# Two graph-attention layers on one core: rank products, list counting, row scatters and the last block's small tile moved

## The chip, the cores and the metric

The kernel runs on one core of one Trainium2 chip. The metric is the device time of one execution in microseconds (us). Before the change the median of three runs is 1944.09 us (1942.63 to 1948.15). The profile is of one further execution of 1946.15 us, whose recorded span, from the first to the last instruction, is 1944.3 us.

## The reference

Two layers of the same form are applied to 2708 tokens of width 512, in float32, with an adjacency matrix of 0 and 1 that has some eight neighbours in a row:

```
mask   = adj + eye(n)
q,k,v  = h @ Wq.T + bq, h @ Wk.T + bk, h @ Wv.T + bv      # 8 heads of 64
scores = q . k / sqrt(64), -1e9 where mask == 0
ctx    = softmax(scores) @ v
h1     = layer_norm(h + ctx @ Wo.T + bo)
h2     = layer_norm(h1 + relu(h1 @ W1.T + b1) @ W2.T + b2)  # hidden width 2048
```

All tokens pass through every product; attention needs only the few neighbours of a token.

## The kernel before

**Tiles.** Tokens are handled in 22 tiles of 128; the last (number 21) has 20 tokens. Products of such a small tile are made as "quarters": four products share the array, each in 32 of the output's 128 partitions, and the vector engine adds the four parts (`plus_rest`, L583).

**Keys, values and lists.** `first` (L832) makes keys and values of layer 0, tile by tile, adds the key bias on the vector engine (L879) and writes the rows to a table in memory (L885). Beside this, `lists` (L670) finds for each token the places of its neighbours in the adjacency matrix. `counted` (L699) counts every token's list and sums the counts over the tiles, some 30 vector-engine instructions ending with L746; before, it is called as soon as the last tile's lists are made, in the loop over the tiles.

**Ranks.** Tokens are then regrouped by length of list, so that a tile needs as many steps as its longest list. `ranked` (L756) turns the counts into places: four products (L763, L770) over a triangular matrix and a matrix of ones, a multiply and a sum on the vector engine (L777, L783), and a conversion (L785). With the places, GpSimd scatters the lists tile by tile to memory (L789, 22 indirect transfers), reads them back in the new order (L808, L801), and takes from them the old number of each new token (`ident_i`, L819). `own_rows` (L961) then gathers rows of the input for the first tiles of attention; TensorE transposes them and makes their queries (`own_query`, L972). Gathers of keys and values (L1004) follow.

**Queries.** `first_queries` (L903) makes the queries of layer 0 for all tiles (L922), which the vector engine scales and adds the bias to (L929), and which are written to memory. In it `ranked` is called after the first tile's product. After tile 12, `listed(True)` (L834) makes the first lists of places usable (L827), and at tile 13 the own queries are made.

**Attention and feed-forward.** Tiles are worked in 11 pairs (`blocks`, L1432), the last being the small tile 21 with tile 8. `attend` (L1437) multiplies gathered keys by the query on the vector engine, takes the exponential on the scalar engine and adds up weighted values; it is advanced step by step inside the loops of feed-forward. `feed_forward` (L1311) makes 16 chunks of the hidden layer (L1351), applies ReLU on the scalar engine (L1359), and adds each chunk into one accumulator per tile (`second`, L1324), three chunks late (`LAG`); for a small tile `quarters` (L1339) does this once per four chunks. Then come the sum with the residual (L1375), the norm (`norm`, L1147, with one power on GpSimd), and in the last layer a scatter of the rows to the output (L1379). In layer 0, `keys_values` (L1390) makes the next layer's keys and values and scatters them to the next table (L1417).

**Order.** The orders of TensorE, of the scalar engine and of SP's transfer queue are as written. GpSimd's is as written up to the last block of layer 0; the vector engine's only in `first_queries` and at the start of layer 1. Elsewhere a planner orders these two when the kernel is built. Two writes to one table are put in order by default: the later one waits on GpSimd until the earlier has landed. For the rank scatters this is declared needless already:

```
tc.declare_no_dep(move.ins, group="moved", reason="no two tokens have one rank")
```

Of the kernel before, what the change touches and what calls it, by code (L numbers as in the profile page):

```python
# [18 lines left out]
P = 128  # L19
# [453 lines left out]
def by_edges(ctx: ExitStack, tc: tile.TileContext, x, xT, adj, layers, out, good):  # L473
# [130 lines left out]
    def lists_of(pa):  # L604
# [151 lines left out]
        def ranked(hot, before, half):  # L756

            at = pa.tile([P, NT], F32, tag="at", name="at", bufs=1)
            for h in range(2):
                ts = slice(h * half, (h + 1) * half)  # L760
                pr = ps.tile([P, DM], F32, tag="g", name="pr")
                w = half * LIST
                nc.tensor.matmul(  # L763
                    pr[:, :w],
                    tri,
                    hot[:, ts, :].rearrange("p t e -> p (t e)"),
                    start=True,
                    stop=False,
                )
                nc.tensor.matmul(  # L770
                    pr[:, :w],
                    ones,
                    before[:, ts, :].rearrange("p t e -> p (t e)"),
                    start=False,
                    stop=True,
                )
                nc.vector.tensor_tensor(  # L777
                    hot[:, ts, :].rearrange("p t e -> p (t e)"),
                    hot[:, ts, :].rearrange("p t e -> p (t e)"),
                    pr[:, :w],  # L780
                    ALU.mult,
                )
                nc.vector.tensor_reduce(at[:, ts], hot[:, ts, :], AX.X, ALU.add)  # L783
            ranks = pa.tile([P, NT], I32, tag="ranks", name="ranks", bufs=1)
            nc.vector.tensor_copy(ranks, at)  # L785
            moved = []
            for t in range(NT):
                r = size(t)
                move = nc.gpsimd.indirect_dma_start(  # L789
                    out=rec_d[:, :],  # L790
                    out_offset=bass.IndirectOffsetOnAxis(ap=ranks[:r, t : t + 1], axis=0),
                    in_=rec[:r, t, :],
                    in_offset=None,
                    bounds_check=N - 1,
                    oob_is_err=False,
                )
# [11 lines left out]
            rest = nc.gpsimd.dma_start(out=new[:LW, last, :], in_=rec_d[last * P :, :])  # L808
# [10 lines left out]
            nc.gpsimd.tensor_copy(ident_i[:, first:], new[:, first:, LIST])  # L819
# [12 lines left out]
    def first(w, meanwhile):  # L832
# [39 lines left out]
        for t in range(NT):  # L872
# [4 lines left out]
            if t == 0:  # L877
                finish(turning)
            nc.vector.tensor_tensor(kv[:r, :DM], k[:r], bk[:r], ALU.add)  # L879
            plus_rest(kv[:r, :DM], k, r)  # L880
            v = project(xs, r, wv, "v", other=True)
            nc.scalar.copy(kv[:r, DM:], v[:r])
            plus_rest(kv[:r, DM:], v, r)
            if before:
                nc.scalar.dma_start(**before)  # L885
            before = dict(out=kv_d[0][t * P : t * P + r, :], in_=kv[:r])
            if t == 0:
                finish(load())
            while done < min(NT, 1 + LEAD * t):
                lists(done)  # L890
                done += 1
                if done == NT:
                    counts = counted()
            meanwhile(t)
            if t == QT:
                wq = matrix(w, "Wq", "wq")
# [6 lines left out]
    def first_queries(bq, wq, counts, ranked, listed, pa, tokens, meanwhile):  # L903
# [14 lines left out]
        for t in range(NT):  # L918
# [1 line left out]
            if t % 2 == 0 and made:  # L920
                written()
            q = project(tokens(t, 1), r, wq, "q", other=t % 2 > 0)  # L922
            if t == 0:
                ranked(*counts)
                xrs = [own_rows(g) for g in order[:3]]
            if t % 2 == 0:
# [45 lines left out]
    def own_query(g, zT, to, bq, wq):  # L972
# [3 lines left out]
        nc.vector.scalar_tensor_tensor(to[:r], q[:r], DK**-0.5, bq[:r], ALU.mult, ALU.add)  # L976
        plus_rest(to[:r], q, r, DK**-0.5)

    def checked():

        sc = at.tile([P, LIST, NH], F32, tag="sc", name="checks", bufs=2)
# [19 lines left out]
            nc.sync.dma_start(out=to[:r], in_=table[g * P : g * P + r, :])  # L1001

    def gather(to, table, s):
        nc.gpsimd.indirect_dma_start(  # L1004
            out=to,
            out_offset=None,
            in_=table[:, :],
# [106 lines left out]
            return cx  # L1114

    places = []

    def rows_of_keys(n):

# [12 lines left out]
    def loads(n):  # L1132

        ready = []
        for g, s0, c in (chunk for g in order for chunk in chunks_of(g)):
            r = size(g)
            kv = rows_of_keys(n)
            for s in range(s0, s0 + c):
                gather(kv[:r, s - s0, :], kv_d[n], idx[:r, g, s : s + 1])
            ready.append(kv)  # L1140
            if len(ready) > EARLY:
                yield ready.pop(0)
# [32 lines left out]
    class Layer:  # L1175
# [135 lines left out]
        def feed_forward(self, block, hs, hT):  # L1311

            w = sum(size(g) for g in block)
            accs = [ps_a.tile([P, DM], F32, tag=f"a{i}", name=f"a{i}") for i in range(len(block))]
            fts = []

            def second(f, only=None):
                c0 = 0
# [29 lines left out]
            for f in range(NFC):  # L1348
                pf = ps_f.tile([P, DM], F32, tag="f", name="pf")
                for c in range(NC):  # L1350
# [20 lines left out]
            zs = []  # L1371
            for g, a, h in zip(block, accs, hs):
                r = size(g)
                z = h
                nc.vector.tensor_tensor(z[:r], a[:r], h[:r], ALU.add)  # L1375
                plus_rest(z[:r], a, r)
                norm(z, r, self.g2, self.e2)
                if self.n == NL - 1:
                    nc.gpsimd.indirect_dma_start(  # L1379
                        out=out,  # L1380
                        out_offset=bass.IndirectOffsetOnAxis(ap=ident_i[:r, g : g + 1], axis=0),
                        in_=z[:r],
                        in_offset=None,
                        bounds_check=N - 1,
                        oob_is_err=False,
                    )
                zs.append(z)
            yield zs

        def keys_values(self, block, zs):  # L1390
# [23 lines left out]
                yield  # L1414
            for i, g in enumerate(block):
                r = size(g)
                nc.gpsimd.indirect_dma_start(  # L1417
                    out=kv_d[n][:, :],
                    out_offset=bass.IndirectOffsetOnAxis(ap=ident_i[:r, g : g + 1], axis=0),
                    in_=kvs[:r, i, :],  # L1420
                    in_offset=None,
                    bounds_check=N - 1,
                    oob_is_err=False,
                )
            yield

# [280 lines left out]
```

## Time and profile before

| what | value |
|---|---|
| median of three runs | 1944.09 us |
| profiled execution, its span | 1946.15 us, 1944.3 us |
| TensorE busy | 1858.4 us, 96% of the span |
| vector engine busy | 1321.0 us, 68% |
| scalar engine busy | 934.7 us, 48% |
| GpSimd busy | 809.3 us, 42% |
| mean granted TensorE clock | 0.981 |
| transfers | 366.92 MB, mean 189 GB/s |

PE is TensorE, PEld its weight load, DVE the vector engine, ACT the scalar engine, POOL GpSimd, SP the engine that only issues transfers. A line of the time line gives the start, the length, the engine, the line in the kernel, the operation, what it writes and reads, and how many instructions in a row are merged; in brackets stands the idle time of the engine before it and what ended it. Lengths of neighbouring lines can overlap, as instructions are pipelined. A float32 product shows as two instructions (passes). The granted clock is 1 at full speed.

### The profile page before, as it was taken

How to read it: one execution, taken by the hardware profiler on the slowest of the kernel's cores; microseconds unless marked ns; L12 is line 12 of the kernel's file. 1: busy time of each engine (PE TensorE's matmuls, PEld its weight loads, DVE VectorE, ACT ScalarE, POOL GpSimd, SP SyncE). 2: the span in 40 equal slices, each digit the busy share in tenths (PEclk: the TensorE clock that was granted, in tenths of full speed). 3: DMA queues.
4: the chain of work that ended last, by engine and by line, in shares of the span. 5: the costliest groups of instructions: out<-in, count | busy, mean ns of one | idle time of the engine just before them, and what ended most of it. 6: DMA issues, size and time to landing. Idle time of an engine off the chain costs nothing. (4 is left out here: it accounts for less than half of the span.)

```text
span 1944.3 us, 20898 instructions
## 1 busy us (share of the span) xinstructions
PE 1858.4 (96%) x6162; PEld 1096.7 (56%) x6162; DVE 1321.0 (68%) x2172; ACT 934.7 (48%) x3219; POOL 809.3 (42%) x710
## 2 busy tenths in 40 slices
PE   9998968999999999999999997999999999999996
PEld 4443435556656556665665553566666666666663
DVE  5885467768759687695841237696987998877421
ACT  4660236445546655574451113555475767654510
POOL 3113526535536555364410124344555775546101
PEclk9999979999999999999999998999999999999998
DMA  9998848555646656554401478656665766643000
GB/s 322 355 314 299 275 136 302 172 179 184 205 138 201 217 188 197 177 183 154 146 17 65 136 246 325 202 197 204 203 222 168 251 222 220 209 155 125 17 6 14
DMA packets 131486, 366.92 MB, mean 189 GB/s; under 512 B 16668, under 2 KB 37004, under 8 KB 128654
## 3 DMA queue, kind: packets, MB, share of 16 engines
q0 software_dynamic: 69120, 246.35, 38.0%
q1 hardware_dynamic: 53332, 99.66, 14.8%
q10 hardware_dynamic: 8910, 19.48, 2.6%
q8 instruction: 50, 0.82, 0.2%
q14 instruction: 74, 0.61, 0.1%
HBM read 314.62 MB, written 50.83 MB: 188 GB/s over the span
## 5 line engine op out<-in xcount | busy, mean ns | idle before, releaser
L1004 POOL DMA_INDIRECT kv<-kv_d,idx x420 | 547.0, 1302 | 452.2 <-DVE acc L1080 273.5
L1351 PE MATMUL pf<-hT,w 128*128 128x256 f32 (+1 forms) x2816 | 637.2, 373 | 7.2 <-ACT ft L1359 5.2
L1324 PE MATMUL a<-w,ft 128*128 128x512 f32 x1344 | 632.2, 596 | 5.3 <-ACT ft L1359 4.4
L1351 PEld LDWEIGHTS pf<-hT,w 128*128 128x128 f32 x2816 | 521.2, 191 | 186.6 <-issue 106.5
L1359 ACT ACTIVATE ft<-pf,b 128x256 f32<-128x256 f32 (+1 forms) x352 | 160.3, 460 | 458.5 <-PE pf L1351 458.3
L1041 DVE TENSOR_TENSOR kv<-kv,q 128x1024 f32<-128x1024 f32 (+3 forms) x222 | 254.2, 1157 | 169.2 <-DMA kv<-kv_d,idx 131.1
L1324 PEld LDWEIGHTS a<-w,ft 128*128 128x128 f32 x1344 | 253.2, 191 | 198.6 <-issue 171.6
L1067 ACT ACTIVATE kv<-kv,p 128x64 f32<-128x64 f32 x1232 | 311.0, 335 | 5.0
L1047 DVE TENSOR_REDUCE sc<-kv 128x16 f32<-128x1024 f32 (+3 forms) x222 | 253.8, 1153 | 1.5
L1080 DVE TENSOR_TENSOR acc<-acc,kv 128x1024 f32<-128x1024 f32 (+2 forms) x178 | 204.0, 1146 | 18.9 <-ACT kv L1067 17.0
L1156 POOL TENSOR_TENSOR rd<-va,mhalf 128x1 f32<-128x1 f32 (+1 forms) x88 | 90.4, 1028 | 274.6 <-DVE va L1154 273.7
L576 PE MATMUL o<-wo,cT 128*128 128x512 f32 x336 | 151.1, 602 | 0.5 <-ACT cT L1171 0.5
L1073 DVE TENSOR_TENSOR kv<-kv,p 128x512 f32<-128x512 f32 (+1 forms) x178 | 121.4, 682 | 34.6 <-ACT p L1060 34.6
L1060 ACT ACTIVATE p<-sc,minus 128x8 f32<-128x8 f32 x420 | 102.8, 294 | 69.2 <-DVE sc L1047 62.1
L1111 ACT ACTIVATE cx<-acc,su 128x64 f32<-128x64 f32 (+1 forms) x352 | 88.5, 334 | 74.7 <-DVE su L1103 57.6
L576 PEld LDWEIGHTS o<-wo,cT 128*128 128x128 f32 x336 | 64.5, 193 | 83.2 <-issue 72.9
L681 ACT ACTIVATE code<-aj 128x2708 bf16<-128x2708 int32 (+1 forms) x22 | 73.3, 3332 | 49.2 <-POOL aj L677 49.0
L684 DVE MAX8 tops<-code 128x8 f32<-128x247 f32 (+2 forms) x242 | 83.1, 401 | 19.3 <-ACT code L681 19.3
L1160 DVE SCALAR_TENSOR_TENSOR h<-h,rd,ln_b 128x512 f32<-128x512 f32 (+1 forms) x88 | 65.6, 747 | 40.6 <-POOL rd L1156 40.6
L1067 ACT ACTIVATE acc<-kv,p 128x64 f32<-128x64 f32 (+1 forms) x352 | 88.8, 334 | 1.4
L1410 ACT COPY kvs<-v 128x512 f32<-128x512 f32 (+1 forms) x22 | 12.9, 586 | 158.9 <-PE v L576 138.5
L1375 DVE TENSOR_TENSOR h<-a,h 128x512 f32<-128x512 f32 (+1 forms) x44 | 29.9, 679 | 85.2 <-PE a L1339 48.8
(154 smaller groups left out, 1560.2 us busy)
## 6 DMA issues: line engine op xcount, KB each, us to landing
aj<-in_adj SPq DMA_DIRECT2D x21, 1354.0 KB, 8.4
kv_d<-kvs ACTq DMA_DIRECT2D x21, 512.0 KB, 7.4
w<-in_W SPq DMA_DIRECT2D x20, 512.0 KB, 6.5
xg<-in_xT SPq DMA_DIRECT2D x19, 512.0 KB, 8.6
kv<-kv_d,idx POOLq DMA_INDIRECT x420, 5.8
w<-in_W ACTq DMA_DIRECT2D x12, 512.0 KB, 7.2
q_d<-qs SPq DMA_DIRECT2D x22, 256.0 KB, 3.4
zT_d<-zT SPq DMA_DIRECT2D x22, 256.0 KB, 4.3
```

The lines of the kernel that those rows point to most:

```text
L576: nc.tensor.matmul(o[:r], xs(c), wm[:, c, :], start=(c == 0), stop=(c == NC - 1))
L1004: nc.gpsimd.indirect_dma_start(out=to, out_offset=None, in_=table[:, :], in_offset=bass.IndirectOffsetOnAxis(ap=s, axis=0), bounds_check=N ...
L1041: nc.vector.tensor_tensor(kv[:r, :c, :DM], kv[:r, :c, :DM], self.q[:r].unsqueeze(1).to_broadcast([r, c, DM]), ALU.mult,)
L1047: nc.vector.tensor_reduce(self.sc[:r, s0 : s0 + c, :], kv[:r, :c, :DM].rearrange("p s (h d) -> p s h d", d=DK), AX.X, ALU.add,)
L1060: nc.scalar.activation(p[:r, s, :], self.sc[:r, s, :], AF.Exp, bias=minus[:r, g, s : s + 1])
L1067: nc.scalar.activation(to[:, i, hd], kv[:r, i, DM + h * DK : DM + (h + 1) * DK], AF.Copy, scale=p[:r, s0 + i, h : h + 1],)
L1073: nc.vector.tensor_tensor(to[:, 0, :].rearrange("p (h d) -> p h d", d=DK), kv[:r, 0, DM:].rearrange("p (h d) -> p h d", d=DK), p[:r, s0, : ...
L1080: nc.vector.tensor_tensor(self.acc[:r, :c, :], self.acc[:r, :c, :], kv[:r, :c, DM:], ALU.add)
L1156: nc.gpsimd.tensor_tensor(rd[:r], va[:r], mhalf[:r], ALU.pow)
L1324: nc.tensor.matmul(a[:r], fts[f][:, c0 : c0 + r], self.w2[f // 2][:, f % 2, :], start=(f == 0), stop=(f == NFC - 1),)
L1351: nc.tensor.matmul(pf[:, :w], self.w1[f // 2][:, c, f % 2 * P : f % 2 * P + P], hT[:, c, :w], start=(c == 0), stop=(c == NC - 1),)
L1359: nc.scalar.activation(ft[:, :w], pf[:, :w], AF.Relu, bias=self.b1[:, f : f + 1])
```

## The change

Four things are changed.

1. `counted` is called in the last turn of the loop over key tiles, behind that tile's key bias and value copy and ahead of the additions of its quarters. Before, it was called when the last lists had been made, some turns earlier.
2. `ranked` is called after the second tile's query product, not the first's. Its two output banks are those of the feed-forward accumulators (`ps_a`, tags a0 and a1) and no longer taken in turn with the queries' (`ps`, tag g).
3. The scatters of key and value rows, and of output rows, go through a new function `put`, which declares that they need no order among themselves. The first gather from a table is made to wait for all its scatters by hand.
4. In the last block of the last layer (`apart`) all 16 hidden chunks are made first and kept, in two tiles of the pool of gathered keys; the quarters of the small tile run after every fourth chunk. The small tile's sum, norm and scatter are written first, and the 16 products of the full tile after them.

```
-                pr = ps.tile([P, DM], F32, tag="g", name="pr")
+                pr = ps_a.tile([P, DM], F32, tag=f"a{h}", name="pr")
...
             nc.vector.tensor_tensor(kv[:r, :DM], k[:r], bk[:r], ALU.add)
-            plus_rest(kv[:r, :DM], k, r)
             v = project(xs, r, wv, "v", other=True)
             nc.scalar.copy(kv[:r, DM:], v[:r])
-            plus_rest(kv[:r, DM:], v, r)
             if before:
                 nc.scalar.dma_start(**before)
+            if t == NT - 1:
+                counts = counted()
+            plus_rest(kv[:r, :DM], k, r)
+            plus_rest(kv[:r, DM:], v, r)
...
                 lists(done)
                 done += 1
-                if done == NT:
-                    counts = counted()
...
             q = project(tokens(t, 1), r, wq, "q", other=t % 2 > 0)
-            if t == 0:
+            if t == 1:
                 ranked(*counts)
                 xrs = [own_rows(g) for g in order[:3]]
...
+    def put(table, s, rows, group):
+
+        move = nc.gpsimd.indirect_dma_start(
+            out=table[:, :],
+            out_offset=bass.IndirectOffsetOnAxis(ap=s, axis=0),
+            in_=rows,
+            in_offset=None,
+            bounds_check=N - 1,
+            oob_is_err=False,
+        )
+        tc.declare_no_dep(move.ins, group=group, reason="no two tokens have one place")
+        tc.add_to_no_dep_group(group, move.ins)
+        return move
...
+                load = gather(kv[:r, s - s0, :], kv_d[n], idx[:r, g, s : s + 1])
+                for move in written[n]:
+                    tc.add_manual_dep(
...
+                written[n].clear()
...
+            apart = self.n == NL - 1 and block == blocks[-1]
...
-                ft = dn.tile([P, 2 * P], F32, tag="ft", name="ft", bufs=4)
+                if apart:
+                    ft = wide[f // 8][:, f % 8, :]
+                else:
+                    ft = dn.tile([P, 2 * P], F32, tag="ft", name="ft", bufs=4)
...
-                if f >= LAG:
+                if f >= LAG and not apart:
                     second(f - LAG)
...
-            for g in block:
+            if apart:
+                quarters(NFC - 1)
+            for g in () if apart else block:
...
                 r = size(g)
+                if apart:
+                    for f in range(NFC):
+                        second(f, g)
                 z = h
                 nc.vector.tensor_tensor(z[:r], a[:r], h[:r], ALU.add)
...
-                    nc.gpsimd.indirect_dma_start(
...
+                    put(out, ident_i[:r, g : g + 1], z[:r], "out")
...
-                nc.gpsimd.indirect_dma_start(
...
+                written[n].append(
+                    put(kv_d[n], ident_i[:r, g : g + 1], kvs[:r, i, :], f"kv{n}")
                 )
```

More of the change, by code (lines that the diff above doesn't have):

```diff
@@ L1003, in gather @@
     def gather(to, table, s):
-        nc.gpsimd.indirect_dma_start(
+        return nc.gpsimd.indirect_dma_start(
             out=to,
@@ L1116, in by_edges @@
     places = []
+    written = [[] for _ in range(NL)]
     def rows_of_keys(n):
@@ L1138, in loads @@
             for s in range(s0, s0 + c):
-                gather(kv[:r, s - s0, :], kv_d[n], idx[:r, g, s : s + 1])
+                load = gather(kv[:r, s - s0, :], kv_d[n], idx[:r, g, s : s + 1])
+                for move in written[n]:
+                    tc.add_manual_dep(
+                        load.ins,
+                        move.ins.name,
+                        mybir.DependencyInfo(
+                            mybir.DependencyClass.Sync, mybir.DependencyReason.DATA
+                        ),
+                        reason="every row of keys is in its place",
+                    )
+                written[n].clear()
             ready.append(kv)
@@ L1315, in feed_forward @@
             fts = []
+            apart = self.n == NL - 1 and block == blocks[-1]
+            if apart:
+                wide = [
+                    at.tile([P, SLOTS, 2 * DM], F32, tag="kv", name="fts", bufs=KVB)
+                    for _ in range(2)
+                ]
+                wide = [t.rearrange("p s (i w) -> p (s i) w", w=2 * P) for t in wide]
             def second(f, only=None):
@@ L1373, in feed_forward @@
                 r = size(g)
+                if apart:
+                    for f in range(NFC):
+                        second(f, g)
                 z = h
@@ L1378, in feed_forward @@
                 if self.n == NL - 1:
[L1379 to L1386, printed above, removed]
+                    put(out, ident_i[:r, g : g + 1], z[:r], "out")
                 zs.append(z)
@@ L1416, in keys_values @@
                 r = size(g)
[L1417 to L1423, printed above, removed]
+                written[n].append(
+                    put(kv_d[n], ident_i[:r, g : g + 1], kvs[:r, i, :], f"kv{n}")
                 )
```

## The prediction

> **What bounds the kernel now.** I read the page's head, then who TensorE waited for, then the order of events at the three places that the change touches. From the page, and from TensorE's list of waits (total, times, longest, in us):
>
> ```profile
> PE 1858.4 (96%) x6162; PEld 1096.7 (56%) x6162; DVE 1321.0 (68%) x2172; ACT 934.7 (48%) x3219; POOL 809.3 (42%) x710
> PE tp L1166 <- ACT cx L1111: 25.5, 4, 14.2
> ...
> PE q L576 <- DVE kvs L879: 6.1, 1, 6.1
> ...
> PE tp L1166 <- DMA xr<-in_x,ident_i: 0.3, 1, 0.3
> ```
>
> TensorE sets the time nearly everywhere. Its idle time is 86 us, and from 1230 us to 1925 us it waits only 4.5 us in all. So a faster GpSimd or vector engine in the middle buys nothing; only the start (lists, ranks, first attention), the boundary of the layers and the tail can move the end. The start, in order of time (start, length, engine and line, in brackets the idle time before and what ended it):
>
> ```profile
> 160.83 0.71 DVE L746 TENSOR_TENSOR before<-before,run 128x528 f32<-128x528 f32 x1
> 161.46 1.87 DVE L879 TENSOR_TENSOR kvs<-k,bk 128x512 f32<-128x512 f32 x3
> 162.20 6.43 PE L576 MATMUL q<-wq,xg 128*128 128x512 f32 x8 [6.07 <-DVE kvs L879]
> 168.47 0.61 PE L763 MATMUL pr<-hot,tri 128*128 128x264 f32 x2
> 169.56 0.43 DVE L777 TENSOR_TENSOR hot<-hot,pr 128x264 f32<-128x264 f32 x1 [1.92 <-PE pr L770]
> 171.85 1.10 POOL L789 DMA_INDIRECT rec_d<-rec,ranks  x1 [20.29 <-DVE ranks L785]
> 172.70 0.69 DVE L929 SCALAR_TENSOR_TENSOR qs<-q,bq 128x512 f32<-128x512 f32 x1 [1.14 <-DMA kv_d<-kvs]
> 203.05 0.59 POOL L808 DMA_DIRECT2D new<-rec_d  x1 [3.05 <-DMA rec_d<-rec,ranks]
> 209.00 1.10 POOL L1004 DMA_INDIRECT xr<-in_x,ident_i  x1 [0.65 <-POOL ident_i L819]
> 215.32 1.85 PE L1166 MATMUL tp<-ident,xr 128*128 128x128 f32 x12 [0.28 <-DMA xr<-in_x,ident_i]
> 227.51 0.69 DVE L929 SCALAR_TENSOR_TENSOR qs<-q,bq 128x512 f32<-128x512 f32 x1 [2.13 <-PE q L576]
> 263.15 1.91 PE L1166 MATMUL tp<-ident,cx 128*128 128x128 f32 x4 [14.21 <-ACT cx L1111]
> ```
>
> Three things to see. The key biases (L879) run behind the counting (L746), and TensorE loses 6.07 us to that. From the rank products at 168.47 a chain without play leads on: ranks, 22 scatters on GpSimd at 1.28 us each, the lists back, the rows of the first own queries, and their transposes at 215.32, which already wait 0.28 us. And the next big pause, 14.21 us, is for attention that starts from the same lists. The tail:
>
> ```profile
> 1923.86 0.68 DVE L1375 TENSOR_TENSOR h<-a,h 20x512 f32<-20x512 f32 x1 [28.02 <-PE a L1339]
> 1926.01 0.69 DVE L1375 TENSOR_TENSOR h<-a,h 128x512 f32<-128x512 f32 x1
> 1931.96 1.16 POOL L1379 DMA_INDIRECT out<-h,ident_i  x1 [0.57 <-DVE h L1160]
> 1936.58 1.01 POOL L1379 DMA_INDIRECT out<-h,ident_i  x1 [3.47 <-issue]
> ```
>
> Both norms of the last block share the vector engine, and the second scatter stands 3.47 us with nothing to do but see the first land.
>
> **What the Trainium skill says.** "TensorE: Matmul & The Clock Gate", What's actually happening: after about one idle window of 3.4 us the array falls to half rate until it has been busy for a window. The trace agrees: after the pause of 6.07 us eight passes took 6.43 us, where tiles of eight passes are 3.43 us apart later. "DMA: Bandwidth & Descriptors", Anatomy of one DMA: a transfer has about 2 us of fixed cost, mostly the receipt of the write; here a row scatter of the output lands 2.7 to 3.8 us after issue, so that is what a wait between two scatters costs. "TensorEngine Tiling (Array Packing)", Key Properties: changing the tiling mode drains the array; here the quarter products (20-row tile) begin 0.09 us after the last product's modelled end, 0.5 us later than the next load would have.
>
> **The change part by part.** The changed kernel can be built, so the order of its instructions on each engine is known.
>
> Counting behind the key biases: on the vector engine nothing moves. Its order there is the planner's; in the changed build the two full biases and the small one still follow the last add of the counting. The 6.07 us pause and the half-rate query behind it stay: 0. (If it had moved, up to 6 us plus some 3 us of half clock were to be had.)
>
> Rank products behind the second query: they stay ready before 168.47, so nothing is gained by waiting; they move back by one query, 3.43 us, and the multiply (169.56) could start at 172.99. But the vector engine has a fixed order here, and the scaling of query 0 now stands ahead of it. That waits for the write of the last keys to leave its buffer, which held until 172.70, and takes 0.69 us: the multiply starts at 173.4, 3.85 us later. Ranks, 22 scatters, lists back, own rows and key gathers (213.36) all follow on GpSimd in order: +3.85 each. TensorE's pause of 0.28 us becomes about 4.1. Own rows may land faster than then: before, they shared the queues with a query write and a load issued at 208.93 and 209.39, now these have a head start. Taken: -0.7 (0 to -1.9). A pause near 4 us costs clock: after 3.66 us at 285 the clock stood at 0.5 until about 290.6, after 3.75 us at 658.8 for about 3.5 us; half of 3.5 to 5.4 us is 1.7 to 2.7. The query multiplies behind it are on the path, since the vector engine waits for them (2.13 us at 227.51) before attention's second step. Taken +1.7 (0 to 3.3). Sum +4.8, ends +2 and +7.2. Could the 14.21 us pause absorb this? No: what it waits for is late by the same amount. The two other accumulator banks for the products cost nothing: no query behind the products waited for a bank.
>
> Row scatters independent: in layer 0 the second scatter of a pair mostly waits for the scalar engine's copy of the values, not for the first (403.73 and 409.30; 558.22 and 566.83). At the boundary the last one goes at 1156.05, released by the copy that ends at 1155.77, and the first gather waits 2.59 us for its landing as before. The added waits of that gather on all lanes are semaphore reads of about 0.04 us. In layer 1 GpSimd is freed a little while TensorE has no wait. Taken 0; -1 to +0.5. Were TensorE not full there, a pair could be worth up to 3 us.
>
> Last block: TensorE now does all 16 hidden chunks, each fourth followed at once by quarter products, and then 16 products of the full tile. Before, a full-tile product lay between a hidden chunk and the quarters and covered the ReLU. Chunk 7 of before: products start 1902.59, ReLU 1903.85 to 1904.23. With 0.2 us to wake TensorE the quarters start 1.84 us after the chunk's start and take 0.99: 2.83 us, against 1.007 for a plain chunk. 12 x 1.007 + 4 x 2.83 + 16 x 0.857 + 0.27 (drain) = 37.4 us from 1890.92: TensorE ends at 1928.3, not 1925.65, +2.65. But the small tile's add, norm and scatter now lie under the last 13.7 us of products. For the full tile alone, the block before shows 3.97 us from add (1888.55) to scatter (1892.52); plus 0.2 for two small copies between: add at 1928.45, scatter at 1932.65, instead of 1936.58: -3.9. The 7.7 us from there to the end of the span stay. Ends: -6.6 if the ReLU wait is nothing, -2 if it is nearly twice as long. The hidden tiles lie in key buffers last filled at 1780 us: no wait.
>
> Sum: +4.8 + 0 + 0 - 3.9 = +0.9. The profiled execution took 1946.15 (span 1944.3 and 1.85 around it), so 1947.05; it was 2.06 above the median of the three runs, so against that 1945.0. About 0.3%, 5.8 us, is what can be told from no change.
>
> **Rivals.** (1) Slower, about 1951. The write of the last keys, now ahead of the rank multiply, lands late. It took some 4.5 us from issue (167.67, 0.53 us) to 172.70, where such writes have a median of 7.4; every us later is one more on the chain. At 7.4 it is +2.9, and with the clock at its upper end the start costs 9.3. It decides once the start costs over 9.7. For: the queues are full from 166 to 186 us. Against: what is in flight then is unchanged. (2) Faster, about 1937.5: the rank chain hides its delay, as rows and lists land quickly on queues that then have less to carry, and the ReLU is covered after all: 0 - 6.6. For: the DMA share at 208 to 210 us is only 0.10. Against: transposes wait already. (3) The tail gives nothing, as the ReLU waits eat it: +4.8, 1949; still no difference by the measure.
>
> **How the numbers follow.** The sum above 0.58, rival 1 0.20, rival 2 0.12, rival 3 0.10. Rival 3 and the sum lie inside 0.3% but for a few in a hundred at the slow side; so faster 0.12, same 0.66, slower 0.22. The range for 8 in 10 runs from 1938 (just short of rival 2) to 1951.5 (the ends +7.2 and -2 give +5.2, 1949.3; rival 1 reaches past it).
>
> **What would show it.** Pause before the first query multiply again near 6 us; first rank scatter near 175.7; transposes of own rows waiting near 3 to 4 us with clock 0.5 behind it; first context transposes of the second tile near 268; tail with the last scatter some 7.7 us before the end, no wait before it, and pauses of about 0.5 us ahead of the quarters. The forecast fails if counting does come late on the vector engine, if the own rows don't follow the ranks, or if the last block's pauses are far from 0.6 us each.

## The result and the profile after

In the first comparison, 20 runs of each kernel, the changed kernel took 1942.41 us in the median (1935.73 to 1954.34) and the kernel before 1948.91 (1942.63 to 1956.16): ratio 0.9969, interval 0.9955 to 0.9984, that is 6.0 us less. The forecast was no change; this is just over the 0.3% that it called the bound, and the interval leaves out 1. The profiled execution took 1944.02 us, its span 1942.3.

One thing stands ahead of all else. The kernel before took 1948.91 us here; three of these 20 runs are the ones that the forecast started from (median 1944.09), and the other 17 have a median of 1949.64. On later occasions it took 1943.0 to 1944.1 us four times, on three chips, and 1949.55 once, on another (the first comparison's chip is not on record). The changed kernel took 1942.4 and 1946.5 us where the kernel before was slow, and 1947.3 and 1948.0 where it was fast. Part of what follows is about that.

TensorE of the changed kernel, from the page and from its list of waits (total, times, longest):

```profile
PE 1859.4 (96%) x6162; PEld 1098.8 (57%) x6162; DVE 1321.4 (68%) x2172; ACT 934.0 (48%) x3219; POOL 804.6 (41%) x710
PE tp L1191 <- ACT cx L1125: 26.1, 3, 13.9
PE q L576 <- DVE kvs L879: 5.1, 1, 5.1
PE tp L1191 <- DMA xr<-in_x,ident_i: 2.3, 2, 1.6
```

Nothing large went away: the same pauses stand at the same places, the counting's (5.1 us) among them. The start, from the time line of the changed kernel:

```profile
161.84 8.83 PE L576 MATMUL q<-wq,xg 128*128 128x512 f32 x16 [5.13 <-DVE kvs L879]
172.28 41.36 PE L576 MATMUL q<-wq,xg 128*128 128x512 f32 x96
172.36 0.69 DVE L929 SCALAR_TENSOR_TENSOR qs<-q,bq 128x512 f32<-128x512 f32 x1 [5.08 <-DMA kv_d<-kvs]
172.97 0.42 DVE L777 TENSOR_TENSOR hot<-hot,pr 128x264 f32<-128x264 f32 x1
175.16 1.11 POOL L789 DMA_INDIRECT rec_d<-rec,ranks  x1 [23.96 <-DVE ranks L785]
204.70 0.59 POOL L808 DMA_DIRECT2D new<-rec_d  x1 [1.62 <-DMA rec_d<-rec,ranks]
205.70 2.67 DVE L929 SCALAR_TENSOR_TENSOR qs<-q,bq 128x512 f32<-128x512 f32 x4 [10.60 <-remote]
208.57 1.10 POOL L1018 DMA_INDIRECT xr<-in_x,ident_i  x1 [0.64 <-POOL ident_i L819]
215.24 0.63 PE L1191 MATMUL tp<-ident,xr 128*128 128x128 f32 x4 [1.59 <-DMA xr<-in_x,ident_i]
265.15 1.91 PE L1191 MATMUL tp<-ident,cx 128*128 128x128 f32 x4 [13.87 <-ACT cx L1125]
```

The rank multiply (L777) stands behind the scaling of the first query, which waits 5.08 us for the last key write, and the first rank scatter is 3.31 us later than before (175.16 against 171.85). But the gather of own rows is at 208.57, where the profile of the kernel before has it at 209.00: between these two profiles the delay is gone on the way. The scatters' landing is waited for 1.62 us instead of 3.05, and from the reading back of the lists to their first use by the gather pass 3.87 us (204.70 to 208.57) instead of 5.95. Beside it stands a line that the profile of the kernel before did not have: the vector engine's query scalings stand 10.60 us until 205.70, while TensorE makes queries without a break (from 172.28). "Remote" means that this view names no instruction that ended the wait.

The tail of the changed kernel:

```profile
1916.03 14.00 PE L1356 MATMUL a<-w,fts 128*128 128x512 f32 x32
1922.26 0.95 POOL L981 DMA_INDIRECT out<-h,ident_i  x1 [1.10 <-DVE h L1185]
1930.07 0.69 DVE L1415 TENSOR_TENSOR h<-a,h 128x512 f32<-128x512 f32 x1 [8.13 <-PE a L1356]
1934.05 1.03 POOL L981 DMA_INDIRECT out<-h,ident_i  x1 [1.09 <-DVE h L1185]
```

The small tile's scatter (1922.26) lies, with its sum and norm, under the full tile's 14.00 us of products, and the last scatter waits for nothing but its own norm. From the first hidden product of the last block (1893.19) to the last scatter it takes 40.86 us; before, 45.66 (1890.92 to 1936.58). So the tail gave 4.8 in these two profiles. Behind the last scatter 8.24 us pass to the end of the span, where it was 7.75, so some 4.3 arrive; and the unchanged tail itself takes 44.45 to 46.27 us in five profiles, as its wait for the first scatter's landing varies.

### The profile page after: what moved, and what is told of

It reads as the page before. It is cut to its first block, busy times and chain, and to the rows that moved or that the text cites. A ratio compares the mean times of both kernels' runs of the same rounds, so it can differ in the third digit from the quotient of the medians.

```text
span 1942.3 us, 20878 instructions
## 1 busy us (share of the span) xinstructions
PE 1859.4 (96%) x6162; PEld 1098.8 (57%) x6162; DVE 1321.4 (68%) x2172; ACT 934.0 (48%) x3219; POOL 804.6 (41%) x710
## 4 chain that ended last, share of the span: by engine, by line
PE 48%; issue 3%; DVE 3%; DMA 1%; POOL 1%; ACT 1%; POOLq 0%; SPq 0%; DVEq 0%
PE pf L1383 19%; PE a L1356 18%; PE o L576 4%; PE q L576 2%; PE k L576 1%; PE v L576 1%; PE tp L1191 1%; DVE kv L1055 1%; POOL kv L1018 1%; DVE sc L1061 1%; DMA kv<-kv_d,idx 1%; PE a L1371 1%; DMA q<-q_d 0%; DVE acc L1094 0%; POOL rd L1181 0%
## 5 line engine op out<-in xcount | busy, mean ns | idle before, releaser
L1356 PE MATMUL a<-w,ft 128*128 128x512 f32 x1312 | 615.0, 595 | 6.1 <-ACT ft L1394 3.6
L1394 ACT ACTIVATE ft<-pf,b 128x256 f32<-128x256 f32 (+1 forms) x336 | 153.8, 463 | 432.7 <-PE pf L1383 428.8
L1356 PEld LDWEIGHTS a<-w,ft 128*128 128x128 f32 x1312 | 247.8, 191 | 196.5 <-issue 169.3
L1087 DVE TENSOR_TENSOR kv<-kv,p 128x512 f32<-128x512 f32 (+1 forms) x178 | 121.2, 681 | 36.1 <-ACT p L1074 36.1
```

Of the source, the lines that this page charges most:

```text
L1087: nc.vector.tensor_tensor(to[:, 0, :].rearrange("p (h d) -> p h d", d=DK), kv[:r, 0, DM:].rearrange("p (h d) -> p h d", d=DK), p[:r, s0, : ...
L1356: nc.tensor.matmul(a[:r], fts[f][:, c0 : c0 + r], self.w2[f // 2][:, f % 2, :], start=(f == 0), stop=(f == NFC - 1),)
```

## First experiments: each part alone

The theories: A, the tail makes the gain and the start comes out even; B, the start makes a gain of its own, as the lists came back early; C, the scatters' lost order makes it; D, the parts simply add up; E, late ranks cost nothing when the other parts are in place. All kernels of this section ran on one chip, 22 runs each, beside 75 of the kernel before (median 1943.7).

**The tail alone** (the kernel before with the fourth part; the scatters keep their order):

```
+            apart = self.n == NL - 1 and block == blocks[-1]
-                if f >= LAG:
+                if f >= LAG and not apart:
                     second(f - LAG)
...
+                if apart:
+                    for f in range(NFC):
+                        second(f, g)
```

> Kernel before with the fourth part alone: the last block's hidden chunks first, the small tile finished first. Row and output scatters stay in order, counting and rank products where they were. Theory A (the tail makes the whole gain, the start comes out even): 4 to 6 us faster than before, last scatter about 41 us after the first product of the last block instead of 45.7. Theory B (the start makes the gain and the tail is worth no more than its 3.9 us on paper or less): 2 to 4 us faster. Theory C (the scatters' lost order makes it): within 2 us, as here the order stays.

Measured: 0.9979 [0.9967, 0.9992], -4.1 us. The tail took 40.85 us, as in the changed kernel. The step of -3.9 holds.

**The rank part alone** (parts 1 and 2):

```
-            if t == 0:
+            if t == 1:
                 ranked(*counts)
...
-                if done == NT:
-                    counts = counted()
+            if t == NT - 1:
+                counts = counted()
```

> Kernel before with the first two parts alone: counting called behind the last biases, rank products behind the second query and in the accumulators' banks. Theory A: within 1.5 us of before, with the first rank scatter some 3.5 us later and the lists back no more than 1 us later, as the wait for the scatters' landing shrinks. Theory B: 2 to 4 us faster. My prediction's step: 4.8 us slower.

Measured: 1.0033 [1.0020, 1.0046], +6.4 us. The time line of this kernel:

```profile
207.39 0.59 POOL L808 DMA_DIRECT2D new<-rec_d  x1 [4.16 <-DMA rec_d<-rec,ranks]
216.38 0.63 PE L1166 MATMUL tp<-ident,xr 128*128 128x128 f32 x4 [1.93 <-DMA xr<-in_x,ident_i]
218.33 1.09 PE L1166 MATMUL tp<-ident,xr 128*128 128x128 f32 x4 [1.32 <-DMA xr<-in_x,ident_i]
223.27 1.09 PE L1166 MATMUL tp<-ident,xr 128*128 128x128 f32 x4 [3.85 <-DMA xr<-in_x,ident_i]
```

Here the delay isn't made up: the lists are read back at 207.39, and TensorE waits three times for own rows, 7.10 us in all; the trace has its clock at 0.50 for 10.24 us from 218.18. Against the kernel before the first scatter is 3.36 us later (175.21), the reading back 4.34. This is the loss that the forecast gave to the ranks, larger by a third.

**The scatters alone** (part 3; the last block as before):

```
+        tc.declare_no_dep(move.ins, group=group, reason="no two tokens have one place")
+        tc.add_to_no_dep_group(group, move.ins)
```

> Kernel before with the third part alone: scatters of key rows and output rows unordered among themselves. The last two output scatters then need not wait for one another: by the profile of before that is about 3.2 us at the end. Theory A: 2.5 to 3.5 us faster, all of it at the end, nothing in the middle. Theory C: 4 us faster or more, as pairs of scatters in the middle count too. Theory B: as A, since this is the tail's wait alone.

Measured: 0.9989 [0.9977, 1.0001], -2.1 us, not quite told from none, and less than the 2.5 to 3.5 expected. Its tail took 42.50 us, 3.2 less than before: the second output scatter no longer stands 3.47 us for the first to land. In the layers' middle nothing moved.

**Parts 3 and 4 without the rank part** (the changed kernel with the two edits of the ranks taken back):

> Changed kernel with counting and rank products put back to their old places and banks; scatters and last block as changed. Theory A: 4 to 6 us faster than before, the same as the changed kernel within 1.5 us. Theory B: only 2 to 4 us faster. My prediction's step: 4.8 us faster than the changed kernel, so about 10 us faster than before.

Measured: 0.9973 [0.9961, 0.9984], -5.3 us. The tail took 40.85 us, no less than with the tail part alone, so the scatters' 3.2 and the tail's 4.8 are not two gains: once the small tile is out early there is no second scatter to wait. Under D the changed kernel should then come to 6.4 - 5.3 = +1.1 us. It had measured -6.0.

## Second: the changed kernel again, and three versions that mend its start

All on another chip; the kernel before took 1944.05 (49 runs).

> The changed kernel as it is, beside the others on one chip. Theory D (the parts add up: rank products +6.4 us, scatters and tail together -5.3): within 2 us of before. Theory E (with the other parts in place the late ranks cost nothing, as the first comparison says): 5 to 7 us faster than before, and a profile in which the lists are back as early as before (about 208 us) though the scatters end 3 us later.

Measured, 13 runs: 1947.29 us, 1.0018 [1.0006, 1.0030], +3.5 us. The same kernel that had gained 0.31% lost 0.18%; the intervals don't meet. In this profile the lists come back late, as with the rank part alone: reading back at 207.16 after a wait of 4.51, transposes of own rows waiting 2.13 and 1.12 us, contexts of the second tile at 268.42 (265.15 in the first comparison).

The next three ask whether the loss can be mended. The first forces, in the last four turns of the key loop, the vector engine to the order in which the lines are written, so that the biases do come ahead of the counting:

```
+            if t == NT - 4:
+                hand.enter_context(tc.manual_schedule(engines={mybir.EngineType.DVE}))
```

> Changed kernel with the vector engine's order in the last four turns of the key loop as written, so that the last biases do run before the counting. Pause of TensorE before the first query multiply: 6 us to under 1 us. The counting ends some 3 us later, and the ranks stay behind the key write's landing, so first rank scatter within 2 us of the changed kernel's. Theory D and E alike: TensorE then waits longer for the first own rows (up to 9 us instead of 3 to 7), and the total is within 2 us of the changed kernel. If the pause itself is what counts, 6 to 9 us faster than the changed kernel.

Measured: 1.0021 [1.0008, 1.0033], level with the changed kernel, as D and E expected. Its time line:

```profile
161.25 0.68 DVE L882 TENSOR_TENSOR kvs<-k,bk 20x512 f32<-20x512 f32 x1 [6.93 <-DMA kv_d<-kvs]
169.40 1.25 PE L770 MATMUL pr<-before,ones 128*128 128x264 f32 x2 [4.81 <-DVE before L746]
191.76 8.57 PE L576 MATMUL q<-wq,xg 128*128 128x512 f32 x13 [5.05 <-DMA xg<-in_xT]
```

The pause ahead of the first query is gone, but the small tile's bias waits 6.93 us for a key write to free its buffer, with the whole counting queued behind it; TensorE then waits 4.81 us at the rank products and 5.05 us for an input load. The pause was moved, not removed. The first rank scatter is at 179.58, 4.75 us later than in the changed kernel on this chip, where at most 2 had been expected. So the counting edit, which by itself moved nothing on the vector engine (with and without it TensorE's pause ahead of the first query is 4.6 to 6.1 us), won nothing when its order was forced in this way.

The second version puts the scaling of the first two queries behind the rank multiplies as well, which takes the wait for the key write off the rank chain; the third adds one full-tile product ahead of each set of quarters in the last block, to cover the ReLU:

```
-            if t == 1:
+            if t == 0:
+                q0 = q
+            if t == 1:
                 ranked(*counts)
+            for i, o in [] if t == 0 else [(0, q0), (1, q)] if t == 1 else [(t % 2, q)]:
...
+                if apart and f % 4 == 0 and f:
+                    quarters(f - 1)
```

> As the one before, and the scalings of the first two queries put behind the rank multiplies, which then need not wait for the last keys' write to land. First rank scatter 4 to 6 us earlier than in the changed kernel (about 169 to 171 us), own rows and first attention as much earlier. If the chain from ranks to first attention sets the start: 5 to 8 us faster than the changed kernel. If the late ranks cost nothing (theory E): within 2 us of it.

> As the one before, and in the last block one more product of TensorE ahead of each set of quarters, so that they no longer wait for the ReLU: 4 pauses of about 0.5 us gone, the last scatter some 39 us after the block's first product instead of 41. 1.5 to 2.5 us faster than the one before; 10 us or more faster than the kernel before if the rank chain sets the start.

Measured: 1.0010 [0.9998, 1.0022] and 0.9998 [0.9989, 1.0008]. The second version missed its expectation: the first rank scatter came at 175.38, not at 169 to 171, as the vector engine mixes the six additions of the small tile's quarters in with the rank multiplies and sums (169.84 to 175.07). The covered ReLU took the tail from 40.86 to 38.76 us. All of this together only brings the kernel back to where it was without the change.

## Third: rank part and the rest on one chip

On a third chip, the kernel before at 1943.03 (42 runs):

> The changed kernel, measured a third time, now beside the kernel without its rank part. Theory D (the parts add up: ranks about +6.4 us, scatters and tail about -5.3): ratio 1.0005, between 0.999 and 1.002, and 5 to 8 us slower than g2. Theory E (with the other parts in place late ranks cost nothing, so that the first comparison, 0.9969, was the true one): 0.997, level with g2. If it falls on a third value while g2 stays, the start of this kernel varies from chip to chip by more than one comparison's interval.

> The changed kernel without parts 1 and 2, as in e4. Both theories: 0.997 again (-5 to -6 us); what tells is its distance to g1: 5 to 8 us under D, below 2 us under E.

> g2 with one more TensorE product ahead of each set of quarters in the last block, which covers the ReLU. Tail, first hidden product of the last block to the last scatter: 38.8 us against 40.86 in g2. Time 2 us less than g2: ratio 0.9962, some 7.3 us under the kernel before, and the fastest of all runs. If the tail shortens and the time doesn't, something after the last scatter sets the end.

> The kernel before with parts 1 and 2 alone, as in e2. Theory D: 1.0033 again (+6.4 us), the same distance to before as g1 has to g2. If it comes out near 1.000 here, the cost of late ranks belongs to a chip and not to the change.

| kernel | ratio, interval | against before |
|---|---|---|
| changed kernel | 1.0022 [1.0011, 1.0032] | +4.3 us |
| without the rank part | 0.9959 [0.9945, 0.9974] (6 runs) | -8.0 us |
| the same, ReLU covered | 0.9973 [0.9961, 0.9984] | -5.2 us |
| rank part alone | 1.0032 [1.0019, 1.0045] | +6.2 us |

The rank part alone costs what it did, and no less with the other parts in place: the changed kernel stands 0.0063, 12 us, over the one without it, or 0.0044, 8.6 us, if the later 0.9978 of the latter on the same chip is taken, which rests on 20 runs. Theory E falls here. D gives 6.2 less 4.3 to 8.0, that is -1.8 to +1.9, and the measured +4.3 lies above it, as the +3.5 before lay above D's +1.1. So the parts may not simply add up; with intervals of some 2 us to either side on each term this isn't settled. Covering the ReLU shortened the tail again (1890.62 to 1929.38, 38.76 us, against 40.86), but the times don't show the 2 us: the two kernels' intervals overlap, and the covered one's median is even the higher. That expectation is missed or can't be told, with only six runs of the one. Nothing behind the last scatter takes the gain in the profiles: from the block's first hidden product to the end of the span they take 47.04 us against 48.86.

## Fourth: the place of the rank products, and a chip like the first

On a fourth chip the kernel before took 1949.55 us (59 runs), as in the first comparison. The first kernel is the changed one with the products back behind the first query; the second has them behind the fourth (t == 3 in the same place):

```
-            if t == 1:
+            if t == 0:
                 ranked(*counts)
```

> The changed kernel with the rank products behind the first query again; the edit of the counting and the other banks stay. If the cost of the ranks is the place of the products alone (my step, counting at nothing): as e4 and g2, ratio 0.9965 (0.9950 to 0.998), first rank scatter 3 to 4 us earlier than in h3. If the counting edit or the banks carry it: as the changed kernel, 1.002.

> The rank products behind the fourth query, two queries (6.9 us) later than in the changed kernel. If lists, own rows and attention follow the ranks one for one: 5 to 8 us slower than h3, ratio about 1.005 to 1.006, lists back 5 to 7 us later. If the queues take the delay up: level with h3.

> The changed kernel beside h1. Parts that don't hide each other: ratio 1.002 as in f0 and g1, and 8 us or so slower than h1. If the first comparison, 0.9969, comes back on this chip, gain and loss belong to the chip.

Measured, 22 runs each: 0.9980 [0.9969, 0.9992] behind the first query, 0.9981 [0.9971, 0.9991] behind the second (the changed kernel), 1.0020 [1.0009, 1.0031] behind the fourth. So on this chip the gain came back, and, as E has it, the place of the products, first or second query, made no difference (the medians are 1948.35 and 1946.51; the runs of the former fall in two groups, see the last section). Later still costs: two more queries, 6.9 us of TensorE, cost 0.0039, 7.6 us.

Why did it cost nothing here? In the profiles of this chip and in that of the first comparison, and in none of the others, the writes of the queries (SP, L912) stop for 12 to 16 us around the end of the rank scatters although TensorE goes on making queries; this is called the write stop below. (In the three versions of the second section 13 to 15 us lie between two writes as well, but there TensorE itself makes no query for 4.3 to 5.1 us, as it waits for an input load.) The kernel with the products behind the first query:

```profile
185.69 0.37 SPq L912 DMA_DIRECT2D q_d<-qs  x1
196.30 0.69 DVE L929 SCALAR_TENSOR_TENSOR qs<-q,bq 128x512 f32<-128x512 f32 x1 [10.64 <-PE q L576]
...
198.92 0.59 POOL L808 DMA_DIRECT2D new<-rec_d  x1 [1.59 <-DMA rec_d<-rec,ranks]
200.54 2.49 DVE L929 SCALAR_TENSOR_TENSOR qs<-q,bq 128x512 f32<-128x512 f32 x4 [3.56 <-remote]
201.26 0.37 SPq L912 DMA_DIRECT2D q_d<-qs  x1
...
208.94 8.80 PE L576 MATMUL q<-wq,xg 128*128 128x512 f32 x16 [3.41 <-DMA xg<-in_xT]
```

From 185.69 to 201.26 no query is written, where elsewhere one write follows the other by 6.87 us. The write, of two tiles, waits for the scalings at 196.30 and 200.54, and the first of these for TensorE's product. The loads of inputs (L844) are issued behind these writes, so they are late too (186.16, then 201.72); TensorE waits 3.41 us for one and then runs 16 passes in 8.80 us, of which full speed takes 6.87. The changed kernel on the same chip:

```profile
193.02 0.37 SPq L912 DMA_DIRECT2D q_d<-qs  x1
...
203.96 0.60 POOL L808 DMA_DIRECT2D new<-rec_d  x1 [1.61 <-DMA rec_d<-rec,ranks]
206.34 0.37 SPq L912 DMA_DIRECT2D q_d<-qs  x1
```

Its rank scatters begin 5.06 us later (174.27 against 169.21), and one more write gets out, at 193.02, with a load behind it; no wait for an input load is left in its list of waits.

How fast the lists come back goes with the load on the queues. In the four profiles with the write stop the transfer engines are busy to 7 or 8% in the last 2 us of the scatters and to 8% at most in the 1.6 us behind, and the lists are read 1.6 us after the last scatter. In nine profiles they are busy to 84 to 92% ahead of that end and to 7% at most behind it, and it takes 2.8 to 3.1 us. In the other seven, all with late ranks, a query write and an input load issued 1 to 4 us ahead of that end are still on their way behind it (57 to 100%), and it takes 3.9 to 4.7 us. From the first rank scatter to the gather of own rows it is 33.4 to 34.9 us with the write stop and 36.1 to 38.6 without.

Yet within this chip GpSimd passes the delay on in full: the gather of own rows is at 203.00 with the products behind the first query and at 208.00 behind the second. What makes the 5 us free is TensorE. With the early ranks it takes up the own rows at 217.58 only, 14.58 us after their gather, because of the late input load and the half clock behind it; with the late ranks it takes them up at 214.52, waiting 1.66 and 0.98 us for them.

The sums: from the first rank scatter to the contexts of the second tile the kernel with the products behind the first query takes 95.71 us here (264.92 - 169.21), against 90.4 to 91.6 in the eight profiles of kernels with early ranks and no write stop, so the write stop costs it 4 to 5 us in this profile. The changed kernel takes 92.43 here, against 93.59 and 92.23 without the write stop: it loses nothing. (The rank part alone has the same start and takes 92.4 to 97.1 us, so one profile of late ranks says no more than that.) With the write stop, then, early ranks lose about what late ranks lose without it.

What remains of the gain on this chip, about 0.2%, is the size of what the tail gave alone (0.9979).

**The kernel before, with a profile of its own.** The last three were to show the write stop in the kernel before itself. They ran on the third chip again, where it doesn't occur:

> The kernel before, unchanged, for a profile of it on the same chip: ratio 1.000. On a chip with the pause in the query writes: median near 1949, the pause of 12 us or more shows, and TensorE then waits 3 us or more for an input load and runs at half clock behind it, as in h1. On a chip without it: median near 1943.5 and none of these.

> The kernel before with parts 1 and 2 alone. On a chip with the pause: the late ranks cost nothing, since the pause sets the start: ratio 0.999 to 1.001, not 1.0033. On a chip without it: 1.0033 again.

> The changed kernel without parts 1 and 2. On a chip with the pause: 0.998, as h1, level with the changed kernel there (0.9981). On a chip without it: 0.9965 as in e4 and g2.

Measured, against 1944.13 us: 1.0003 [0.9990, 1.0015], 1.0037 [1.0021, 1.0052] and 0.9978 [0.9968, 0.9987]. The query writes of all three keep their distance of 6.87 us. So the third measurement of the rank part alone gives +7.2 us and of the rest alone -4.3; that the kernel before has the write stop where it takes 1949 us, and loses its 5.5 us there, was not seen in a profile of it. It is argued from the kernel with the products behind the first query: up to 230 us TensorE, the vector and scalar engines and GpSimd run the same instructions in the same order in both.

## Why the prediction was wrong, step by step

The step that failed is the "chain without play" from the ranks to TensorE: that own rows follow the ranks one for one, and that TensorE stands ready for them, so that its "pause of 0.28 us becomes about 4.1". Up to the scatters the step held: multiply at 172.97 (forecast 173.4), first scatter at 175.16 (175.7). Behind them the +4.8 did not come about. Where the write stop occurs (the two kernels of the fourth section on one chip), the rows of late ranks come 5.00 us later and meet a TensorE that takes them up earlier (214.52 against 217.58), since early ranks there have play: TensorE is held by an input load. So the changed kernel lost nothing there. And by the argument of the fourth section the kernel before lost some 5 us that its profile didn't have: the forecast took the start of that profile for granted, without naming this as a risk. For the kernel before itself this loss is not shown.

Rival 2, which got 0.12, had lists and rows that land quickly on emptier queues, and that is what the profile shows (1.62 us instead of 3.05). But its other half, the covered ReLU, did not come about, it forecast 1937.5, and what emptied the queues, the write stop, was nowhere in the profile of before. That the measured time fell between the sum and rival 2 is therefore partly luck of the occasion: two of six had the write stop.

Without the write stop the step was right and a third to a half too small: +6.4, +6.2 and +7.2 us where +4.8 stood. Own rows did follow the scatters there (36.2 to 37.5 us behind the first one in the kernels with the rank part, 36.6 to 37.2 in those with early ranks). The term that is too small lies behind them, in what the wait for own rows and the clock cost. It was taken as one pause of about 4 us with 3.5 to 5.4 us of half clock. With the rank part alone there were three pauses in each profile, 7.10, 6.42 and 3.39 us in all, and in the first of them 10.24 us of half clock; the last, with 3.41 us of half clock, is no more than forecast although its kernel cost the most, so how the surplus divides is open.

The other steps:
- Counting, at nothing: right. The pause stands (5.13 us), in the kernel before itself on the third chip too (5.2 us), and when the order was forced the pause went to other places.
- Scatters, at nothing: right as part of the sum, for a reason that the forecast did not give. Alone they shorten the end by 3.2 us, since the second output scatter's wait goes; the tail takes the same wait away.
- Last block, -3.9: measured -4.1 alone; in the first pair of profiles -4.8 to the last scatter, some -4.3 to the end of the span. The sum of the working held: four chunks with their quarters came to 5.73 us where 5.85 stood. Its parts did not: the quarters begin at once behind the last chunk, wait inside for the last ReLU only, and take 1.58 us, not 0.99; and TensorE takes up the last weights 0.06 us behind that ReLU (1897.80, 1897.86), not 0.2. The 0.09 us of the drain counts from the full tile's step of 0.43 us; by the modelled ends the quarters begin 0.07 us ahead.
- The sum, +0.9: on the two chips without the write stop +3.5 and +4.3 us, on the two occasions with it -6.0 and -3.7. None of the four is +0.9; that they lie to both sides of it does not make the forecast right on any of them.

## What to carry to other kernels

Find out whether a delay is passed on: follow it through every landing behind it to the engine that sets the time, and ask whether that engine would be ready any earlier. Where an effect of a few tenths of a per cent decides, compare on more than one chip, since an interval over runs of one chip says nothing of the next one. And take a change of several parts apart: here the tail alone, without the rank part, is the better kernel wherever it was measured without the write stop (with the scatters' part, 0.9973, 0.9959 and 0.9978 against 1.0018 and 1.0022 for the whole), and with the write stop the place of the ranks made no difference.

## What the runs showed of the hardware

The write stop was not expected. In the four profiles that have it, no query is written for 12.1 to 15.6 us while GpSimd scatters the lists, and the next write goes out 0.5 to 4.1 us behind the end of the last scatter, wherever the ranks were put (201.26, 206.34, 207.20, 209.56 us). In windows of the time line (busy time of each engine, then clock, share of the transfer engines and GB/s), first the kernel with the products behind the first query, on the chip with the write stop:

```profile
190.00:194.00 4.00, 4.00 (x11) 1.82 (x10) 0.00 (x0) 0.00 (x0) 3.04 (x4) 1.00 0.12 32
194.00:198.00 4.00, 4.00 (x10) 1.71 (x9) 0.69 (x1) 0.00 (x0) 2.72 (x3) 1.00 0.08 17
198.00:202.00 4.00, 4.00 (x11) 1.77 (x10) 1.46 (x3) 0.00 (x0) 2.72 (x3) 1.00 0.07 17
```

and then the one without the rank part, on a chip without it:

```profile
190.00:194.00 4.00, 4.00 (x11) 1.74 (x10) 0.69 (x1) 0.00 (x0) 2.93 (x3) 1.00 0.28 94
194.00:198.00 4.00, 4.00 (x11) 1.85 (x10) 0.69 (x1) 0.00 (x0) 2.85 (x3) 1.00 0.80 243
198.00:202.00 4.00, 4.00 (x11) 1.75 (x10) 0.69 (x1) 0.00 (x0) 1.52 (x3) 1.00 0.39 126
```

Over these 12 us the transfer engines are busy to 9%, in the other kernel to 49%. So it isn't bandwidth that is missing, nor does the trace show a late landing: the marks that it has of the landing of the query write issued at 185.69 are at 188.53 to 188.66. What comes late is the news of TensorE's products. Without the write stop the vector engine scales a query 0.04 us behind the end of its product (176.16 and 176.20 us in a kernel without the rank part). In the kernel above, the products that end at 188.36, 191.80, 195.23 and 198.66 us are scaled at 196.30, 200.54, 201.15 and 201.75, which is 7.9, 8.7, 5.9 and 3.1 us late, while TensorE makes its products at the usual step of 3.43 us. The last signal that the trace records ahead of each of the first two is TensorE's own, 0.02 to 0.03 us before. In the changed kernel of the first comparison the longest such delay is 9.2 us (product ended 196.48, scaled 205.70). Measured from the latest instruction that can have sent it, no other signal of an engine is recorded more than 0.7 us late in these profiles, but for those at the end of the run, and in the sixteen other profiles none is. Why TensorE's signals come late there is open.

The same four profiles lack records: 11603 to 11734 marks of landings, where the others have 13188 to 13197, and 992 to 1009 of TensorE's signals, where the others have 1042 to 1045. That is why their lists of transfers give no time of landing. Whether the missing records and the late signals have one cause is open, and so is whether executions that are not profiled have the write stop: only their times fit it. The times of the kernel with the products behind the first query say that one profile isn't all: they fall in two groups, nine from 1938.6 to 1943.1 us and thirteen from 1945.7 to 1953.7, and the profiled execution (1942.15), which has the write stop, is of the lower.

TensorE's clock fell to 0.5 without any long pause, where the forecast counted half clock behind pauses near 4 us. In the changed kernel on the second chip it fell at 218.13 us, behind a wait of 2.13 us and within one of 1.12, for 6.83 us; in the first comparison at 216.48, behind a wait of 1.59 and within one of 0.75, for 3.41 us.

Of one kernel, the same file, the ratio to before was 0.9969, 0.9981, 1.0018 and 1.0022 on four occasions, with intervals of about 0.0012 to either side.
